# Where the tiles with direct denominators stand in a unit, who may use the denominators' PSUM bank, and the order of a row's value products

## The chip, the cores and the metric

One core of one Trainium2 chip runs the whole kernel. The metric is the device time of one execution in microseconds (us). Three runs of the kernel before took 4312.58, 4318.01 and 4329.15 us; the median is 4318.01 us. One more execution was recorded by the hardware profiler; all durations below are from it.

## The reference

Two graph attention layers over one random adjacency of 2048 nodes, for 8 independent inputs (called batches here) of 2048 x 256, in fp32. Cut to what matters:

```python
# layer 0: 8 heads of 32 columns; scores are a sum of two vectors
x_proj = einsum('bnd,hdf->bhnf', x, W)
e = leaky_relu(e_src[..., :, None] + e_dst[..., None, :], 0.2) + beta * log(adj + 1e-6)
attn = softmax(where(adj > 0, e, lowest), axis=-1)          # 2048 x 2048 per head
x = layernorm(x + (attn @ x_proj, heads joined) @ W_out.T)
# layer 1: one head; scores are a product of two matrices
h1, h2, h3 = x @ W1, x @ W2, x @ W3
e = where(adj > 0, leaky_relu(h1 @ h2.T, 0.2), -1e12)
x = layernorm(x + relu(softmax(e) @ h3))
```

## The kernel before

**Two layers at once.** Layer 0 of batch b+1 and layer 1 of batch b run side by side, b = 0 to 6; layer 0 of batch 0 runs alone first (about 526 us), and layer 1 of batch 7 alone last (about 300 us). The seven stretches between are called batches below. At the start of each, a *seam* (`seam`, line 956) turns layer 0's result into layer 1's inputs.

**Layer 0: units, tiles, strips.** A batch has eight units (four head pairs times two halves of the rows, `unit`, line 796). A unit goes through 16 tiles `jt` of 128 neighbours. For each head of the pair, a tile is made as a 128 x 1024 block of unnormalised attention in a slot of a ring of seven (`ring`, 1 MB each): VectorE takes max(c, re) and multiplies with the mask (`make`, recorded at line 880). TensorE multiplies the tile with the values in four products of 32 columns that run beside each other (`products`, line 442, recorded at line 445; "val"). These narrow products are called *strip* work. The sums of the rows, the denominators, are collected in one of two ways:

- In a *chain* tile, ScalarE first scales the mask (line 399), and GpSimd adds the made tile to a running sum (line 888; "sums"). At the unit's end one strip product with ones, "close", adds it up over partitions.
- A *direct* tile needs neither: VectorE reads the mask as it was loaded, and TensorE does a second strip product ("den") into the same PSUM bank that takes the close.

The list `DIRECT` (line 69) says which tiles are direct: 3, 6, 9, 12 and 15 in every unit of batches 1 to 7. The bank "den" is copied out by `dned` (line 947) after the close, and the next unit's first den product waits for that copy.

**Layer 1: rows.** For each of 16 rows `it` of 128 nodes, TensorE computes scores "e" in four blocks `c` of 512 columns (line 1091), ScalarE writes each through a leaky ReLU into one row buffer `p` (line 1097), VectorE subtracts the mask and takes the maximum (line 1136, "mask"), ScalarE takes the exponential (line 1142), and TensorE transposes the four blocks ("T", line 1165), which ScalarE copies to SBUF into one of four slots `pts` (line 1170). Eight pieces of value products ("acc", line 1184) follow, all into one PSUM bank. This is *full* work. While row it is transposed, the scores of row it+1 take its place in `p`, block by block.

**PSUM.** Two banks, `m0` and `m1`, serve e, T, acc and all of the seam; "val" and "den" have one each, and two pairs hold c. A bank given to a T or an e comes back when ScalarE has copied it out; a bank given to acc comes back only when the row's result has been added to x.

**What sets the order.** A planner written into the kernel (`Sched`, line 576) decides at build time in which order each engine gets its instructions: it simulates the engines with a price for each task, a table of slots for each kind of buffer, and a queue with priorities per engine. The order on each engine is then fixed; on the chip, semaphores hold an instruction until its inputs are there. Full work on TensorE is kept in the order in which the loop at line 1235 creates it. Strip work comes between by `choose_pe` (line 599): it compares the tiles already eaten with a goal, and lets a strip in at a lag over 1.5 tiles where the next full task is marked `easy`, over 4 where it is not, or whenever the next full task is not ready for 0.35 us. Every change between full and strip costs a flat 0.13 us in the plan (`TURN`, line 511). A task marked `lock` (the mask, line 1143) waits in the plan for the end of GpSimd's current instruction.

The order of a row in the seven batches comes from these lines: one T, one piece of acc, one e, one piece of acc, and so on, with the last pieces after the loop.

```python
for c in range(NB):
    turn(it, c)
    if c and b + 1 < B:
        acc(it, 2 * c - 2)
    if more:
        scores(it + 1, c)
    if c and b + 1 < B:
        acc(it, 2 * c - 1)
```

In the last layer 1 (b + 1 == B) all eight pieces of acc follow after the four pairs of T and e.

Of the kernel before, what the change touches and what calls it, by code (L numbers as in the profile page):

```python
# [9 lines left out]
F32 = mybir.dt.float32  # L10
# [8 lines left out]
P = 128  # L19
# [8 lines left out]
def kernel(  # L28
# [37 lines left out]


    J2 = NT // 2
    DIRECT = [[range(NT)] * NP] + [[(3, 6, 9, 12, 15)] * NP] * (B - 1)
    SLOTS = 7  # L70

    const = ctx.enter_context(tc.tile_pool(name="const", bufs=1))
# [306 lines left out]
    class Unit:  # L379
# [67 lines left out]
        def copy_values(self):  # L447


            gat, hp, rh, lo = self.gat, self.hp, self.rh, self.hp % 2 * HP * DH  # L450
            parts = [(rh, self.val)]
            if self.b > 0 and hp == 0:
                if rh == 0:
                    gat.first = chunk.tile([P, BK], F32, tag="pt", name="first", bufs=NB)
                    nc.scalar.copy(gat.first, self.val)
                    parts = []
                else:
                    gat.ht = [whole.tile([P, N], F32, tag="heads", name="ht")]
# [49 lines left out]
            stage(at // (NP * 2), at // 2 % NP, at % 2)  # L508

    LATE = 0.15  # L510
    TURN = 0.13
    WINDOW = 8
    LOW, HIGH, STRICT = -1.0, 1.5, 4.0

    QUEUES = {"ACT": (("copy", 0.0), ("relu", 0.3), ("evict", 0.3), ("ends", 0.4), ("exp", 0.9), ("c", 0.4), ("scale", 0.45), ("norm", 0.25)),
              "DVE": (("zsum", 0.0), ("sum", 0.0), ("tinyr", 0.1), ("tinys", 0.1), ("mask", 0.3), ("tinyd", 0.1), ("stats", 0.2), ("make", 0.3)),
# [4 lines left out]
    class Slots:  # L521
# [6 lines left out]
        def at(self, n=0):  # L528
            return sorted(self.free)[n][0] if len(self.free) > n else None
# [5 lines left out]

        def give(self, end, tag):
            self.free.append((end, tag))

    class Hold:

# [35 lines left out]
    class Sched:  # L576


        def __init__(self):
            self.q = {name: [] for names in QUEUES.values() for name, _ in names}  # L580
            self.clock = {eng: 0.0 for eng in QUEUES}
            self.pe, self.kind, self.full, self.strip, self.close = 0.0, None, [], [], []
            self.work, self.eaten, self.goal = 0.0, 0, lambda w: 0.0

        def add(self, *a, **k):
# [4 lines left out]
        def choose(self, eng):  # L590

            now, cands = self.clock[eng], []
            for rank, (name, wait) in enumerate(QUEUES[eng]):
                if self.q[name]:
                    r = self.q[name][0].ready()
                    if r is not None:
                        cands.append((rank, r, wait))
            if not cands:
                return None
            t = max(now, min(r for _, r, _ in cands))  # L600
            rank, r, wait = min(c for c in cands if c[1] <= t)
# [34 lines left out]
            return v[0], v[1], 0  # L636

        def start(self, t, task):
            for h in task.takes:
                h.take()  # L640
            task.end = t + task.busy + task.late
            for h in task.frees:
                h.done(task.end)
            task.emit()
            if task.after:
                task.after()

        def run(self):

            while True:  # L650
                best = None
                for eng in QUEUES:
                    c = self.choose(eng)
                    if c and (best is None or c[0] < best[0]):
                        best = (c[0], eng, c[1])
                c = self.choose_pe()
                if c and (best is None or c[0] < best[0]):
                    best = (c[0], "PE", c)
                if best is None:
                    break  # L660
                t, eng, what = best
                if eng == "PE":
                    task = getattr(self, what[1]).pop(what[2])
                    kind = "full" if what[1] == "full" else "strip"
                    t += TURN if self.kind not in (None, kind) else 0.0
                    self.kind, self.pe = kind, t + task.busy
                    if kind == "full":
                        self.work += task.busy
                else:
                    task = self.q[what].pop(0)  # L670
                    if task.lock:
                        t = max(t, self.clock["POOL"])
                        self.clock["POOL"] = t + task.busy
                    self.clock[eng] = t + task.busy
                self.start(t, task)
# [75 lines left out]
    ctx.enter_context(tc.manual_schedule(engines={e.engine for e in (nc.sync, nc.scalar, nc.vector, nc.gpsimd)}))  # L751
    next(projections)
    S = Sched()
    bank = Slots(2, ["m0", "m1"])
    ring, mts, pts_s, hts, rows_s = (Slots(n, None, name) for n, name in ((SLOTS, "ring"), (4, "mt"), (4, "pts"), (4, "ht"), (4, "rows")))
    v_s, c_s, pen_s, xs_s = (Slots(n, None, name) for n, name in ((2, "v"), (0, "c"), (1, "pen"), (2, "xs")))

# [51 lines left out]
    def unit(b, hp, rh, vs, vhold):  # L809
# [29 lines left out]
        for jt in range(NT):  # L839
# [68 lines left out]
            if jt in u.direct:  # L908
                def den(jt=jt):
                    e = gat.re[:, 1]  # L910
                    if u.den is None:
                        u.den = pacc.tile([P, BK], F32, tag="den", name="den")
                    u.products(u.den, [e[:, jt, h:h + 1].to_broadcast([P, DH]) for h in u.heads], u.s[jt],
                               jt == min(u.direct), False)
                deps = [u.makes[jt, 0], u.makes[jt, 1]]
                if jt == min(u.direct) and before:
                    deps.append(before.dned)
                t2 = pe("strip", "den", 0.86, lambda _, den=den: den(), deps)
                t2.frees = [slot]
                t = t2  # L920
            count = t

            def eat():
                S.eaten += 1
            t.after = eat
        u.closed = pe("close", "close", 0.86, lambda _: u.products(u.den, [ones] * HP, u.sums, False, True),
                      [u.adds[u.chain[-1], 0], u.adds[u.chain[-1], 1], t])
        if hp == 0 and rh == 0:
            hold = Hold(pts_s, 1)
            E.first_hold = hold  # L930
            u.evicted = S.add("evict", 0.5, u.copy_values, [u.vals[NT - 1]], takes=[hold])
        else:
            n = 4 if hp == 0 else 2
            deps = [u.vals[NT - 1]]
            frees = []
            if hp == 0:
                frees = [E.first_hold]
                deps.append(entries[b - 1].last_tr)
            if hp == HP and rh == 0:
                deps.append(entries[b - 1].last_tr)  # L940
            u.evicted = S.add("evict", 0.55 * n, u.copy_values, deps, frees=frees)
        dn = Hold(hts, 1)

        def dn_copy():
            u.dn = chunk.tile([P, BK], F32, tag="ht", name="dn", bufs=4)
            nc.scalar.copy(u.dn, u.den)
        u.dned = S.add("evict", 0.5, dn_copy, [u.closed], takes=[dn])
# [106 lines left out]
    def layer1(b):  # L1054
# [50 lines left out]
        def soft(it):  # L1105
# [33 lines left out]
            def exp():  # L1139
                p = pbox["p"]  # L1140
                r["den"] = den = small.tile([P, 1], F32, name="den1")
                nc.scalar.activation(p, p, AF.Exp, bias=r["neg"], accum_out=den)  # L1142
# [15 lines left out]
        def turn(it, c):  # L1158
# [8 lines left out]
            def cp(t):  # L1167
                pt = chunk.tile([P, BK], F32, tag="pt", name="pts", bufs=NB)
                r["pts"].append(pt)
                nc.scalar.copy(pt, t)  # L1170
# [64 lines left out]
        for it in range(NT):  # L1235
# [31 lines left out]
        layer1(b)  # L1267
    u = U["last"]
    u.evicted.after = lambda: bank.give(u.evicted.end, "val")
    u.dned.after = lambda: bank.give(u.dned.end, "den")  # L1270
# [34 lines left out]
```

## Time and profile before

| | |
|---|---|
| profiled execution | 4315.08 us, span 4313.3 us |
| median of three runs | 4318.01 us |
| mean granted TensorE clock | 0.985 |
| busy: TensorE, VectorE, ScalarE, GpSimd | 95%, 76%, 68%, 66% of the span |
| one batch (the fourth, 494 us): TensorE, VectorE, ScalarE, GpSimd | 474.88, 407.50, 367.37, 413.33 us |
| one make, one scale, one add | 1.27, 1.14, 2.5 us |
| one mask: beside GpSimd, and in the last layer alone | 3.44, 2.29 us (medians) |
| copies of T and e from PSUM | 0.58 and 0.59 us |

An instruction's busy time on TensorE overlaps the next one's, so the busy share says little about how near TensorE is to its own pace; the distance between the starts of two matmuls does. "PE" is TensorE's products, "PEld" its weight loads, "DVE" VectorE, "ACT" ScalarE, "POOL" GpSimd. A wait is written at the instruction that waited, with the one that released it.

### The profile page before, as it was taken

What the parts mean: (1) busy time and instruction counts of PE and PEld (TensorE: products, weight loads), DVE (VectorE), ACT (ScalarE), POOL (GpSimd) and SP (SyncE); (2) the same over time, 40 slices, a digit from 0 to 9 for tenths busy, and PEclk for the clock granted to TensorE, in tenths of its full rate; (3) what the DMA queues carried; (4) which work ended last, traced back from release to release, by engine and by line L of the source; (5) the groups of instructions that cost most, each with busy time, mean ns of one, the idle gap of its engine ahead of it and who ended that gap; (6) DMA issues with size and microseconds to landing.
All of it is one profiled execution on the core that took longest, in us unless ns stands there. A gap on an engine that the chain in (4) does not pass through costs nothing.

```text
span 4313.3 us, 60790 instructions
## 1 busy us (share of the span) xinstructions
PE 4076.4 (95%) x22704; PEld 2114.0 (49%) x22704; DVE 3297.6 (76%) x3391; ACT 2930.5 (68%) x4148; POOL 2854.5 (66%) x1190
## 2 busy tenths in 40 slices
PE   7899799999999999998999999999999999999999
PEld 4444344445444454444444454444544445445666
DVE  7888698888788778778888787887887887885222
ACT  6522478877767777776777777776777777776454
POOL 0000399987877888877888787987778868876000
PEclk9999899999999999999999999999999999999999
DMA  8888777766555665556566565565655565653111
GB/s 263 276 287 289 243 234 249 230 225 228 190 179 192 199 210 185 188 188 197 185 205 194 184 223 183 197 203 179 209 188 189 185 216 180 198 178 123 59 51 41
DMA packets 346441, 843.66 MB, mean 196 GB/s; under 512 B 49697, under 2 KB 166433, under 8 KB 346145
## 3 DMA queue, kind: packets, MB, share of 16 engines
q1 hardware_dynamic: 346144, 839.77, 59.6%
q8 instruction: 178, 2.92, 0.3%
q14 instruction: 119, 0.97, 0.1%
HBM read 763.76 MB, written 75.37 MB: 195 GB/s over the span
## 4 chain that ended last, share of the span: by engine, by line
PE 54%; ACT 14%; DVE 9%; DMA 7%; issue 4%; POOL 1%; SPq 0%; ACTq 0%; DVEq 0%; POOLq 0%
PE e L1091 17%; PE acc L1184 15%; PE val L445 10%; ACT s L399 6%; DMA mt<-mt_d 6%; DVE p L1136 5%; PE T L1165 4%; PE den L445 4%; DVE s L880 3%; PE h L1041 2%; PE h L1067 2%; ACT p L1097 2%; ACT p L1142 2%; ACT pts L1170 1%; POOL sums L888 1%
## 5 line engine op out<-in xcount | busy, mean ns | idle before, releaser
L888 POOL TENSOR_TENSOR sums<-sums,s 128x1024 f32<-128x1024 f32 x1008 | 2488.5, 2507 | 248.2 <-DVE s L880 207.6
L880 DVE SCALAR_TENSOR_TENSOR s<-c,re,s 128x1024 f32<-128x1024 f32 x1232 | 1507.0, 1273 | 112.5 <-ACT c L829 58.6
L399 ACT ACTIVATE s<-mt,re 128x1024 f32<-128x1024 f32 x1232 | 1366.4, 1145 | 185.1 <-DMA mt<-mt_d 92.3
L445 PE MATMUL val<-s,v 128*32 128x512 f32 x8192 | 1036.2, 601 | 36.4 <-DVE s L880 12.2
L1184 PE MATMUL acc<-h,pts 128*128 128x256 f32 x4096 | 1031.9, 385 | 27.0 <-ACT p L1097 26.5
L1091 PE MATMUL e<-x1t,h 128*128 128x512 f32 x2048 | 1000.1, 613 | 20.7 <-ACT pts L1170 17.9
L1184 PEld LDWEIGHTS acc<-h,pts 128*128 128x128 f32 x4096 | 747.4, 191 | 372.6 <-issue 231.7
L1136 DVE CUSTOM_DVE_ANT_0 p<-p,pen 128x2048 f32<-128x2048 f32 x128 | 460.4, 3597 | 533.0 <-ACT p L1097 532.8
L880 DVE SCALAR_TENSOR_TENSOR s<-c,re,mt 128x1024 f32<-128x1024 f32 x560 | 692.9, 1275 | 63.3 <-PE den L445 25.9
L1091 PEld LDWEIGHTS e<-x1t,h 128*128 128x128 f32 x2048 | 363.2, 192 | 424.7 <-issue 274.0
L1097 ACT ACTIVATE p<-e 128x512 f32<-128x512 f32 x512 | 303.7, 593 | 381.8 <-PE e L1091 379.1
L445 PEld LDWEIGHTS val<-s,v 128*32 128x32 f32 x8192 | 232.7, 109 | 568.3 <-issue 446.2
L888 POOL TENSOR_TENSOR sums<-s 128x1024 f32<-128x1024 f32 x112 | 270.4, 2436 | 263.2 <-DVE s L880 254.0
L445 PE MATMUL den<-s,re 128*32 128x512 f32 x3264 | 442.5, 595 | 0.0
L1165 PE MATMUL T<-ident,p 128*128 128x128 f32 x2048 | 325.3, 283 | 92.7 <-ACT p L1142 67.2
L1142 ACT ACTIVATE p<-p,neg 128x2048 f32<-128x2048 f32 x128 | 256.2, 2001 | 197.0 <-DVE neg L1137 196.9
L1165 PEld LDWEIGHTS T<-ident,p 128*128 128x128 f32 x2048 | 238.4, 142 | 306.9 <-ACT p L1142 98.0
L1170 ACT COPY pts<-T 128x512 f32<-128x512 f32 x512 | 296.7, 580 | 89.3 <-PE T L1165 88.6
L413 DVE SCALAR_TENSOR_TENSOR s<-c_in,re,mt 128x1024 f32<-128x1024 f32 x256 | 310.5, 1278 | 52.0 <-DMA mt<-mt_d 39.4
L286 POOL PARTITION_ALL_REDUCE top<-top x8 | 6.6, 820 | 429.6 <-DVE top L285 414.6
L445 PEld LDWEIGHTS den<-s,re 128*32 128x32 f32 x3264 | 107.7, 110 | 239.5 <-issue 235.8
L277 ACT COPY v<-proj 128x512 f32<-128x512 f32 x64 | 37.2, 585 | 192.8 <-PE proj L275 144.5
(100 smaller groups left out, 2467.9 us busy)
## 6 DMA issues: line engine op xcount, KB each, us to landing
mt<-mt_d SPq DMA_DIRECT2D x992, 512.0 KB
c_in<-c_d SPq DMA_DIRECT2D x64, 1024.0 KB
pen<-pen_d SPq DMA_DIRECT2D x112, 512.0 KB
xg<-in_x_dram SPq DMA_DIRECT2D x60, 512.0 KB
adj_t<-in_adj_dram SPq DMA_DIRECT2D x16, 1024.0 KB
mt_d<-mt SPq DMA_DIRECT2D x32, 512.0 KB
rb<-rec_d SPq DMA_DIRECT2D x128, 128.0 KB
adj_r<-in_adj_dram SPq DMA_DIRECT2D x32, 512.0 KB
```

The lines of the kernel that those rows point to most:

```text
L399: nc.scalar.activation(self.s[jt][:, a], self.mt[jt], AF.Copy, scale=self.gat.re[:, 1, jt, h:h + 1])
L413: nc.vector.scalar_tensor_tensor(s[:, a], self.c[a], self.gat.re[:, 0, jt, h:h + 1], m, ALU.max, ALU.mult)
L445: nc.tensor.matmul(dst[ts(q, DH), :], weights[q % 2], s[:, q % 2, ts(q // 2, BK)], start=start, stop=stop)
L880: nc.vector.scalar_tensor_tensor(u.s[jt][:, a], u.c[a], gat.re[:, 0, jt, h:h + 1], m, ALU.max, ALU.mult)
L888: nc.gpsimd.tensor_tensor(u.sums[:, a], of[:, a], u.s[jt][:, a], ALU.add)
L1091: nc.tensor.matmul(t, box["h"][:, kc, ts(it % IG, P)], gat.x1t[:, kc, ts(c, BK)], start=(kc == 0), stop=(kc == KC - 1))
L1097: nc.scalar.activation(pbox["p"][:, ts(c, BK)], t, AF.Prelu, alpha=ALPHA)
L1136: nc.vector.tensor_tensor_reduce(p, p, r["pen"], 1.0, -FMAX, ALU.subtract, ALU.max, neg)
L1142: nc.scalar.activation(p, p, AF.Exp, bias=r["neg"], accum_out=den)
L1165: nc.tensor.transpose(t[:, ts(k, P)], pbox["p"][:, ts(c * IG + k, P)], ident)
L1170: nc.scalar.copy(pt, t)
L1184: nc.tensor.matmul(r["acc"], r["pts"][g][:, ts(k, P)], gat.h3[:, j, :], start=(j == 0), stop=(j == NT - 1))
```

## The change

Four things change in code, and some prices of the planner with them.

1. `DIRECT`: the direct tiles of a unit are 11 to 15 in place of 3, 6, 9, 12 and 15. There are still five, and eleven chain tiles, now 0 to 10.
2. The bank "den" joins `m0` and `m1` in the planner's pool (`Banks`). It may be lent to any T, e, acc or seam task from the moment a unit's last tile has been eaten and `dned` has freed it until tile 8 of the next unit has been eaten; it is taken only when no other bank is free. A unit's first den product then has to take that very bank (`Only`).
3. A row of the seven batches is ordered as in the last layer: T0 e0 T1 e1 T2 e2 T3 e3, then all eight acc. Strips are easy before T0, acc 0 and acc 7.
4. The buffer `first`, which holds the first unit's values for one unit, leaves the four `pts` slots for the four `ht` slots.

In the planner, the change cost between tasks gets a table by pair and only counts where TensorE has no gap; the mask counts as ready only when GpSimd's current instruction is over, so other VectorE work may go first; its price falls from 2.4 to 2.35 us, with 0.5 us of lateness. The function that takes the mask and the minimum's sign is the same in both kernels: the sign is already taken on VectorE (line 1137).

```diff
-    DIRECT = [[range(NT)] * NP] + [[(3, 6, 9, 12, 15)] * NP] * (B - 1)
+    DIRECT = [[range(NT)] * NP] + [[(11, 12, 13, 14, 15)] * NP] * (B - 1)
...
-                    gat.first = chunk.tile([P, BK], F32, tag="pt", name="first", bufs=NB)
+                    gat.first = chunk.tile([P, BK], F32, tag="ht", name="first", bufs=4)
...
-    TURN = 0.13
+    TURN = {False: 0.0, True: 0.14, ("T", "acc"): 0.11, ("acc", "T"): 0.05, ("acc", "e"): 0.08, ("e", "acc"): 0.085, ("T", "e"): 0.04,
+            ("e", "T"): 0.03, ("e", "val"): 0.12, ("T", "val"): 0.13, ("acc", "val"): 0.08, ("val", "e"): 0.19, ("tr", "h3"): 0.1}
+    NOW = [0.0]
+    BACK = 2
...
+    class Banks(Slots):
+        def mine(self):
+            return sorted(f for f in self.free if self.lent or f[1] != "den")
...
+        def take(self):
+            f = self.mine()
+            got = min(f, key=lambda x: (x[0] > NOW[0], x[1] == "den", x[0]))
+            self.free.remove(got)
+            return got[1]
...
+            mask = self.q["mask"][0].ready() if self.q["mask"] else None
+            if False:
+                return None
...
+                        if name == "mask":
+                            r = max(r, self.clock["POOL"])
...
-                    t += TURN if self.kind not in (None, kind) else 0.0
-                    self.kind, self.pe = kind, t + task.busy
+                    if t <= self.pe + 0.05:
+                        t += TURN.get((self.last, task.queue), TURN[kind != self.kind])
+                    self.kind, self.last, self.pe = kind, task.queue, t + task.busy
...
-    bank = Slots(2, ["m0", "m1"])
+    bank = Banks(["m0", "m1", "den"])
...
-                if jt == min(u.direct) and before:
-                    deps.append(before.dned)
+                if jt == min(u.direct):
+                    u.den_hold = Hold(Only(bank, "den"), 1)
+                    t2.takes = [u.den_hold]
...
+                bank.lent = min(u.direct) - BACK > jt + 1 or jt == NT - 1
...
-            hold = Hold(pts_s, 1)
+            hold = Hold(hts, 1)
...
-        u.dned = S.add("evict", 0.5, dn_copy, [u.closed], takes=[dn])
+        u.dned = S.add("evict", 0.5, dn_copy, [u.closed], takes=[dn], frees=[u.den_hold])
...
-            mk = S.add("mask", 2.4, mask, [e.reader for e in r["e"]] + pen, frees=[pen_hold], lock=True)
+            mk = S.add("mask", 2.35, mask, [e.reader for e in r["e"]] + pen, frees=[pen_hold], lock=True, late=0.5)
...
-            t = pe("full", "T", 0.46, tr, [r["exp"]], Hold(bank, 1), ("copy", 0.5, cp, []), easy=(c < 2))
+            t = pe("full", "T", 0.46, tr, [r["exp"]], Hold(bank, 1), ("copy", 0.5, cp, []), easy=(c < 1))
...
-            t = pe("full", "acc", 0.89, mm, deps, hold, easy=(h > 6))
+            t = pe("full", "acc", 0.89, mm, deps, hold, easy=(h == 0 or h == 7))
...
-                if c and b + 1 < B:
-                    acc(it, 2 * c - 2)
...
-                if c and b + 1 < B:
-                    acc(it, 2 * c - 1)
...
-            for h in range(6 if b + 1 < B else 0, 8):
+            for h in range(8):
```

More of the change, by code (lines that the diff above doesn't have):

```diff
@@ L537, in give, with __init__, at, take @@
             self.free.append((end, tag))
+    class Banks(Slots):
+        def __init__(self, tags):
+            super().__init__(len(tags), tags)
+            self.lent = False
+        def mine(self):
+            return sorted(f for f in self.free if self.lent or f[1] != "den")
+        def at(self, n=0):
+            f = self.mine()
+            return f[n][0] if len(f) > n else None
+        def take(self):
+            f = self.mine()
+            got = min(f, key=lambda x: (x[0] > NOW[0], x[1] == "den", x[0]))
+            self.free.remove(got)
+            return got[1]
+    class Only:
+        def __init__(self, slots, tag):
+            self.slots, self.tag = slots, tag
+        def at(self, n=0):
+            return next((f[0] for f in self.slots.free if f[1] == self.tag), None)
+        def take(self):
+            self.slots.free.remove(next(f for f in self.slots.free if f[1] == self.tag))
+            return self.tag
+        def give(self, end, tag):
+            self.slots.give(end, tag)
     class Hold:
@@ L581, in __init__ @@
             self.clock = {eng: 0.0 for eng in QUEUES}
-            self.pe, self.kind, self.full, self.strip, self.close = 0.0, None, [], [], []
+            self.pe, self.kind, self.last, self.full, self.strip, self.close = 0.0, None, None, [], [], []
             self.work, self.eaten, self.goal = 0.0, 0, lambda w: 0.0
@@ L638, in start @@
         def start(self, t, task):
+            NOW[0] = t
             for h in task.takes:
@@ L915, in unit, with eat @@
                 deps = [u.makes[jt, 0], u.makes[jt, 1]]
-                if jt == min(u.direct) and before:
-                    deps.append(before.dned)
                 t2 = pe("strip", "den", 0.86, lambda _, den=den: den(), deps)
                 t2.frees = [slot]
+                if jt == min(u.direct):
+                    u.den_hold = Hold(Only(bank, "den"), 1)
+                    t2.takes = [u.den_hold]
+                    u.den_first = t2
                 t = t2
             count = t
-            def eat():
+            def eat(jt=jt):
                 S.eaten += 1
+                bank.lent = min(u.direct) - BACK > jt + 1 or jt == NT - 1
             t.after = eat
@@ L1269 @@
     u.evicted.after = lambda: bank.give(u.evicted.end, "val")
-    u.dned.after = lambda: bank.give(u.dned.end, "den")
     for a in range(HP):
```

## The prediction

> **What bounds the kernel now.** I read the page's head first, then the busy time by stretches, then the waits, then two pieces of the timeline.
>
> ```profile
> span 4313.3 us, 60790 instructions
> PE 4076.4 (95%) x22704; PEld 2114.0 (49%) x22704; DVE 3297.6 (76%) x3391; ACT 2930.5 (68%) x4148; POOL 2854.5 (66%) x1190
> ...
> 2046.00:2540.00 494.00, 474.88 (x2629) 240.46 (x2628) 407.50 (x420) 367.37 (x508) 413.33 (x173) 1.00 0.60 198
> 4009.00:4313.00 304.00, 292.98 (x1204) 202.82 (x1202) 71.54 (x148) 153.62 (x289) 0.00 (x0) 0.98 0.16 51
> ```
>
> The second pair of lines gives length and then busy time of PE, PEld, DVE, ACT and POOL, first of one batch, then of the last layer. TensorE seems full, but its records overlap, so I take its pace from the last layer, where it runs undisturbed and in the order that the change gives to all batches:
>
> ```profile
> 4151.92 0.60 PE L1165 MATMUL T<-ident,p 128*128 128x128 f32 x4
> 4152.35 1.88 PE L1091 MATMUL e<-x1t,h 128*128 128x512 f32 x4
> 4154.07 0.60 PE L1165 MATMUL T<-ident,p 128*128 128x128 f32 x4
> ...
> 4160.54 7.07 PE L1184 MATMUL acc<-h,pts 128*128 128x256 f32 x32
> 4167.45 1.45 PE L1067 MATMUL h<-x1t,w 128*128 128x512 f32 x3
> ```
>
> By starts, T costs 0.43 us, e 1.72, four pairs 8.62 (4151.92 to 4160.54), eight acc 6.91: 15.53 us a row. A strip product of a tile is spaced 0.86 us. A batch then needs, at this pace: 16 rows, 248.5; eight h1 at 1.72, 13.8; the seam's eight y, h3 and tr, 31; 128 val, 40 den and 8 close strips at 0.86, 151.4. Sum 444.7 us. The seven batches lie between 526 and 4009 us: 3483 / 7 = 497.6 us each. So 53 us a batch, about 375 in all, are lost between TensorE's instructions. I sorted the distances between starts, less the pace: 200 us lie between T, e and acc of a row; 33 us at 349 changes from full to strip (94 ns each) and 108 us at as many changes back (about 95 ns each, and 70 us of real waits at 52 of them, 48 of it before a T); the rest, 34 us, within strips and in the seam. The waits name the causes:
>
> ```profile
> POOL sums L888 <- DVE s L880: 457.3, 119, 13.2
> ...
> PEld e L1091 <- ACT pts L1170: 109.6, 229, 4.5
> ...
> PEld T L1165 <- ACT p L1097: 76.8, 183, 3.4
> ...
> PE T L1165 <- ACT p L1142: 61.8, 29, 11.4
> ...
> PEld acc L1184 <- ACT p L1097: 48.9, 73, 3.4
> ```
>
> An e that waits for `pts`, and a T or acc that waits for `p` of line 1097, wait for a copy to give a bank back. While acc is spread through the row, it holds one of two banks, and T and e share the other. One such wait:
>
> ```profile
> 2002.48 1.03 PE L1184 MATMUL acc<-h,pts 128*128 128x256 f32 x4
> ...
> 2002.92 2.19 ACT L399 ACTIVATE s<-mt,re 128x1024 f32<-128x1024 f32 x2 [2.31 <-DMA mt<-mt_d]
> 2005.02 0.57 ACT L1097 ACTIVATE p<-e 128x512 f32<-128x512 f32 x1
> ...
> 2005.64 0.33 PE L1165 MATMUL T<-ident,p 128*128 128x128 f32 x1 [2.14 <-ACT p L1097]
> ```
>
> ScalarE runs two late scales ahead of e's copy, and TensorE stands for 2.14 us with no second bank.
>
> **What the Trainium skill says.** *Perfetto Trace Analysis*, section Identifying the Most-Contended Engine: the matmul busy share is a bad measure of headroom; the trace agrees, 95% busy against 444.7 of 497.6 us (89%). The same page, Matmuls: independent groups should rotate through PSUM banks, so that the copying of one overlaps the next; the waits above show the lack of it. *TensorEngine Tiling (Array Packing)*, Key Properties: a change of tiling mode drains the array; here strip and full change for 94 + 95 ns. *SBUF — State Buffer*, SBUF: two separate sides: a VectorE instruction with two SBUF inputs and a GpSimd one exclude each other; the mask's median is 3.44 us beside GpSimd, 2.29 in the last layer.
>
> **The change, part by part.** Instructions, bytes and shapes stay: five direct tiles a unit, 20 adds, the same transfers on SP's queue, one `vscale` a pair on POOL (the old run of tiles in steps of three was one instruction too). What changes is order.
>
> *acc in one block.* T and e then have both banks, and the lent third. For the third: T0 e0 T1 fill three banks, and e1 needs T0's, whose copy has had 2.15 us; each later one has at least as long for a copy of 0.6 us. The last layer shows the order with plenty of banks: 7.7 us lost in its 253. With two banks, e(c+1) needs e(c)'s bank, covered only by T, 0.43 us, against 0.20 us until the copy starts (the median), 0.59 of copy and about 0.2 to the next matmul: a stall of 0.55 us. The bank is lent from about tile 1 to tile 8 of 16, so half the time. I take 60% of the 200 us off: -120. Ends: 0 (evictions late in both states) and -170.
>
> *The row's head.* From e3's end to the next T0 the path copy, mask, exponential takes 8.96 us (median). Before, three acc, 2.6 us, and strips covered it; now 6.9 us of acc and strips do. Half of the 48 us before T: -24; ends 0 and -40.
>
> *Strip changes.* The thresholds stay, the easy places go from T0, T1, acc 7 to T0, acc 0, acc 7: about as many clumps. I take a tenth of 349 x 0.19 us: -7; ends +15 and -25.
>
> *The mask's place.* One make, 1.27 us, may now go ahead of it and fill time in which the mask would stand for GpSimd. It lengthens the row's head by up to 1.3 us, hidden by the acc block and the strips; without that cover 112 rows x 1.3 = 146 us. Behind a mask stand makes and z's sum; they gain. 0.
>
> *`first` in `ht`.* For one unit in eight, four `pts` slots in place of three: without it T3's bank would stay taken until two acc have run. It takes a slot from h1, rb and x's loads; 0, end +10.
>
> *Direct tiles last.* This is the cost. ScalarE: a unit has 22 scales at 1.144, 25.2 us, and two c copies, 2.0; all else is 367.4 / 8 less these, 18.7 us. In the eleven chain tiles it needs 25.2 + 2.0 + 11/16 x 18.7 = 40 us of 11/16 x 60.5 = 41.6: full, where before it was evenly at 74%. Copies then come later, and late makes follow. In the half without the third bank, 112 rows x 1/2 x 4 evictions x 0.3 us (a quarter of a scale): +67. I take +65, ends 0 and +240, the latter from the second rival below.
>
> Sum: -120 - 24 - 7 + 65 = -86 us on the profiled 4313.3: span 4227, execution 4229. The median of the runs shown stands 2.9 us above the profiled 4315.08, so 4232 us (-2.0%).
>
> **The rivals.**
>
> *The lost time goes altogether.* With three banks and cover, 444.7 us plus strip changes, 9 us, and seam, 5, is 459 us a batch: -39 x 7 = -270. GpSimd speaks against the whole of it: 413 us busy of 459, 90%. With the favourable ends, -170 - 40 = -210: 4108 us.
>
> *GpSimd runs dry, and the kernel is slower.* Between the make of chain tile 10 and that of the next unit's tile 1 now stand five direct and two chain tiles: 14 makes x 1.275 = 17.9 us, with VectorE's other work (407.5 less 256 makes, 81 of 494 us) 21 us. GpSimd lives from what is waiting to be added. A unit takes it 2733.5 / 56 = 48.8 us of adds and 1.7 of the rest, 50.5 of 62.2 now. So it may idle 11.7 us a unit before it sets the period; the queue at tile 10 must hold at least 9.3 us, almost four adds. Now the adds trail their makes by 2 to 6 us only. If the queue held 7 us, idle would be 14: 56 x 2.3 = +129, 4447; empty, +520. For it: seven ring slots, three or four then held by waiting tiles. Against: eleven chain tiles in a row at 3.8 us against 5 us of adds leave 11 x 1.2 = 13 us waiting by themselves.
>
> *No difference.* Half the time there are two banks, 112 rows x 3 x 0.55 x 1/2 = 92 us of new stalls, and ScalarE's +65: these eat the 151 us. 4318.
>
> *The diff does less than its words.* The sign is on VectorE in both kernels: nothing from it, in any case.
>
> **How the numbers follow.** Forecast, 4150 to 4296: 0.57. All of the gain, under 4150: 0.15. No difference, within 0.5% (22 us, about what a measurement of this kernel can tell): 0.10. Dry GpSimd: 0.18. Faster 0.72, same 0.10, slower 0.18. The range is 4135 to 4345: it leaves out about half of the second case and most of the last, 0.2 together. The likeliest case's own range is 4150 to 4296.
>
> **What would show it.** Right: waits of e on `pts` and of T and acc on line 1097's copy under half of 235 us together; T's wait on the exponential under 40 us; a batch near 485 us; T, e, T, e in all rows. ScalarE's scales bunched, POOL idle about once a unit, in or after tiles 11 to 15. Wrong: POOL's wait for makes well over 457 us with a batch over 498 (the second rival); T and e waiting as long as before, now in the second half of each unit (the third); new waits of scales or makes on ring slots.

## The result, and the profile after

| | median, us | runs | ratio to before (95%) |
|---|---|---|---|
| before | 4317.72 | 20 | |
| after | 4322.78 | 20 | 1.0013 (0.9989 to 1.0037) |

The change makes no difference that can be measured. The forecast was 4232 us, with 4135 to 4345 as range and 0.72 on faster. The measured time lies in the range, but the outcome is "no difference", which the forecast gave 0.10. (Ratios here and below leave out runs more than 1.5% above the fastest of their kernel: two of the twenty after, and eleven of the 22 of one kernel below.)

The two kernels do not lose their time at the same places. In the profiled execution (4324.23 us) the seven stretches, from the first transpose of one seam to that of the next, take 582.8, 489.8, 490.4, 490.0, 476.8, 497.2 and 469.1 us; before they take 512.2, 502.9, 505.2, 493.4, 494.7, 505.4 and 469.3. Six stretches gain 58 us together and the first loses 71. (In the profile before, the first seam's first transpose starts at 536.8 us and the last seam's at 4019.9; the prediction laid the same 3483 us 11 us too early.)

The busy time of the first three stretches of the kernel after (length, then PE, PEld, DVE, ACT, POOL, with TensorE's clock, the share of the DMA engines and GB/s at the end):

```profile
533.00:1116.00 583.00, 509.23 (x2762) 253.00 (x2763) 480.33 (x454) 398.26 (x536) 447.14 (x185) 0.95 0.61 207
1116.00:1606.00 490.00, 468.96 (x2628) 247.13 (x2626) 413.18 (x412) 364.52 (x506) 402.09 (x168) 0.99 0.59 198
1606.00:2096.00 490.00, 470.59 (x2623) 246.16 (x2621) 413.07 (x419) 367.07 (x509) 411.24 (x171) 0.99 0.59 200
```

In the first stretch TensorE stands still for 74 us of 583, and its granted clock falls to 0.95. The waits of the whole kernel after (engine and line, who released it, us in total, times, longest):

```profile
POOL sums L934 <- DVE s L926: 511.7, 77, 20.8
...
DVE s L926 <- ACT s L399: 289.0, 282, 11.1
...
PEld val L445 <- DVE s L926: 135.6, 122, 23.0
...
PE T L1214 <- ACT p L1191: 66.5, 25, 9.5
...
PEld e L1140 <- ACT p L1146: 57.4, 75, 3.6
...
PEld T L1214 <- ACT pts L1219: 26.5, 55, 2.4
...
PEld e L1140 <- ACT pts L1219: 16.8, 20, 0.9
PEld acc L1233 <- ACT pts L1219: 3.5, 10, 0.8
PEld T L1214 <- ACT p L1146: 2.5, 7, 0.8
```

Two things stand out. The waits for a bank fell: the three kinds that came to 235 us before come to 19 now. New ones stand in their place, e behind the copy of the last e (57.4) and T behind the copy of an earlier T (26.5); with these and the small ones on both sides, T, e and acc wait 107 us for copies where they waited 257. That part of the forecast came. And a strip product waits up to 23.0 us for a make, where before the longest wait of a val for a make of this kind was 11.1 us. This is the longest one, in three engines of the timeline:

```profile
639.76 30.07 POOL L934 TENSOR_TENSOR sums<-sums,s 128x1024 f32<-128x1024 f32 x13
...
650.13 21.86 DVE L1185 CUSTOM_DVE_ANT_0 p<-p,pen 128x2048 f32<-128x2048 f32 x1
...
672.11 2.47 DVE L926 SCALAR_TENSOR_TENSOR s<-c,re,s 128x1024 f32<-128x1024 f32 x2
...
645.50 5.83 PE L445 MATMUL val<-s,v 128*32 128x512 f32 x22 [1.30 <-DVE s L926]
673.45 3.06 PE L445 MATMUL val<-s,v 128*32 128x512 f32 x8 [22.12 <-DVE s L926]
```

GpSimd runs thirteen adds without a gap, until 669.8. VectorE's mask starts at 650.13 and needs 2.28 us when it is alone; it takes 21.86, ends 2.2 us after the run has ended, and the makes queued behind it on VectorE start only then. TensorE stands for 22 us. A second mask of 16.3 us, at 591.5, stops TensorE for 17 us in the same stretch. Over the seven stretches, the masks' durations (shortest, median and longest in ns), before and then after:

```profile
L1136 DVE CUSTOM_DVE_ANT_0 p<-p,pen x112: 2281/3440/14412, 599.5 to 3990.6; 128x2048 f32<-128x2048 f32 x112
```

```profile
L1185 DVE CUSTOM_DVE_ANT_0 p<-p,pen x112: 2277/3132/21855, 591.5 to 4000.1; 128x2048 f32<-128x2048 f32 x112
```

The median even falls; the tail grows. A mask alone takes 2.28 us and the rest of one add at most 2.4, so I call a mask over 5 us *passed over*: at least one further add went ahead of it. That happened to 12 of 112 masks before and to 11 after. In all 23 cases the mask came in only when GpSimd's run of adds had come to an end, never at a later boundary inside the run (in two, before, a `vscale` followed that run within 0.5 us and stood behind the mask). In 20 of the 23, what let GpSimd go on, by the releasers that the profile gives, was a VectorE instruction that stood behind the mask, mostly a make: the run ended because GpSimd had nothing left to add. Before, one to five adds went ahead, 2.1 on average; after, up to eight, 3.6 on average. GpSimd's instructions in the seven stretches follow one another without a gap of 0.15 us in runs of 6.8 on average before and 10.4 after. So masks are passed over about as often, and the length of the runs became the price.

### The profile page after: what moved, and what is told of

It is laid out like the page before. It is cut to its first block, busy times and chain, and to the rows that moved or that the text cites. A ratio compares the mean times of both kernels' runs of the same rounds, so it can differ in the third digit from the quotient of the medians.

```text
span 4322.1 us, 60882 instructions
## 1 busy us (share of the span) xinstructions
PE 4045.2 (94%) x22704; PEld 2157.3 (50%) x22704; DVE 3358.5 (78%) x3391; ACT 2914.6 (67%) x4148; POOL 2861.0 (66%) x1190
## 4 chain that ended last, share of the span: by engine, by line
PE 54%; DVE 14%; ACT 10%; issue 7%; DMA 2%; POOL 1%; SPq 0%; ACTq 0%; DVEq 0%; POOLq 0%
PE e L1140 17%; PE acc L1233 13%; PE val L445 11%; DVE s L926 7%; DVE p L1185 5%; ACT s L399 5%; PE den L445 4%; PE T L1214 4%; PE h L1090 3%; PE h L1116 2%; POOL sums L934 1%; ACT p L1146 1%; ACT p L1191 1%; PE y L1031 1%; DMA mt<-mt_d 1%
## 5 line engine op out<-in xcount | busy, mean ns | idle before, releaser
L445 PE MATMUL val<-s,v 128*32 128x512 f32 x8192 | 1047.3, 601 | 95.6 <-DVE s L926 68.5
L1233 PE MATMUL acc<-h,pts 128*128 128x256 f32 x4096 | 924.0, 381 | 0.4 <-ACT pts L1219 0.4
L1233 PEld LDWEIGHTS acc<-h,pts 128*128 128x128 f32 x4096 | 770.0, 190 | 215.5 <-issue 93.2
L926 DVE SCALAR_TENSOR_TENSOR s<-c,re,mt 128x1024 f32<-128x1024 f32 x560 | 678.8, 1274 | 38.5 <-POOL sums L934 28.4
L1185 DVE CUSTOM_DVE_ANT_0 p<-p,pen 128x2048 f32<-128x2048 f32 x128 | 483.1, 3774 | 210.4 <-ACT p L1146 209.4
L1214 PEld LDWEIGHTS T<-ident,p 128*128 128x128 f32 x2048 | 254.5, 144 | 344.5 <-issue 177.3
L1214 PE MATMUL T<-ident,p 128*128 128x128 f32 x2048 | 317.2, 280 | 73.6 <-ACT p L1191 66.5
L1249 ACT ACTIVATE acc<-acc,rec 128x256 f32<-128x256 f32 x128 | 56.7, 443 | 190.7 <-PE acc L1233 184.6
```

What stands on the lines that cost most here:

```text
L445: nc.tensor.matmul(dst[ts(q, DH), :], weights[q % 2], s[:, q % 2, ts(q // 2, BK)], start=start, stop=stop)
L926: nc.vector.scalar_tensor_tensor(u.s[jt][:, a], u.c[a], gat.re[:, 0, jt, h:h + 1], m, ALU.max, ALU.mult)
L1185: nc.vector.tensor_tensor_reduce(p, p, r["pen"], 1.0, -FMAX, ALU.subtract, ALU.max, neg)
L1214: nc.tensor.transpose(t[:, ts(k, P)], pbox["p"][:, ts(c * IG + k, P)], ident)
L1233: nc.tensor.matmul(r["acc"], r["pts"][g][:, ts(k, P)], gat.h3[:, j, :], start=(j == 0), stop=(j == NT - 1))
```

## The experiments

My theory after this comparison: the change gains what it should on TensorE's banks, and gives it back because chain tiles in a row make GpSimd's adds run without a gap, so that a mask that is passed over waits for the end of a long run. Rivals: ScalarE, which now has to scale eleven tiles in a row (the makes' wait for scales rose from 52.7 to 289 us); GpSimd as a bound; and the planner's new place for the mask, which starts 4.6 us after the last copy of e on average where it was 0.1.

All ratios below are to the kernel before, measured beside each kernel, with a 95% interval.

### A GpSimd that stands still for the mask

The edit leaves the order of all other instructions as it is:

```diff
                 nc.vector.tensor_scalar(neg, neg, -1.0, None, ALU.mult)
+                turn_off = small.tile([P, 1], F32, name="yield", bufs=2)
+                nc.gpsimd.tensor_tensor(turn_off, neg, neg, ALU.add)
```

GpSimd reads the mask's result, so its queue stops at this place until the mask is done. I call it the yield. In the kernel after:

> The kernel after, with one small GpSimd instruction behind each mask of the rows (it adds the mask's 128 x 1 result to itself, into a tile that nothing reads), so that GpSimd's queue stops there until the mask is done; the order on all engines is otherwise the same. Theory (the lost gain went into masks that wait while GpSimd runs a long row of adds): no mask over 4.8 us (one of 2.3 plus the rest of one add), no stall of 17 or 23 us in the first of the seven stretches, that stretch near 530 us in place of 583, the whole 50 to 80 us shorter, near 4255. Rival (the scales of eleven chain tiles in a row saturate ScalarE, and the makes wait for them): time unchanged within 10 us, the makes' wait for scales still near 289 us. Second rival (GpSimd is the bound): slower, since it now stands before each mask.

In the kernel before:

> The kernel before, with the same small GpSimd instruction behind each mask. Theory: masks over 4.8 us (41 us beyond that in the profile before, longest 14.4) go, and with them part of the waits before a T: 20 to 40 us shorter, near 4288, less than in the kernel after. Rival (ScalarE): unchanged. Second rival (GpSimd is the bound): slower.

Measured: after with the yield 4214.47 us, 0.9765 (0.9737 to 0.9793); before with the yield 4238.49 us, 0.9818 (0.979 to 0.9846). No mask is passed over in either. The masks of the kernel after with the yield, and the first two of its stretches:

```profile
L1185 DVE CUSTOM_DVE_ANT_0 p<-p,pen x112: 2273/2696/4448, 599.1 to 3885.0; 128x2048 f32<-128x2048 f32 x112
```

```profile
540.00:1089.00 549.00, 511.58 (x2764) 253.15 (x2763) 451.46 (x455) 398.21 (x536) 436.67 (x201) 0.97 0.66 220
1089.00:1560.00 471.00, 462.19 (x2627) 244.55 (x2625) 396.60 (x413) 364.87 (x507) 386.56 (x183) 1.00 0.61 206
```

The wait of its makes for scales:

```profile
DVE s L926 <- ACT s L399: 305.0, 299, 11.0
```

The theory holds and was too small: 108 us from the kernel after, not 50 to 80, and 79 from the one before, not 20 to 40. The first stretch falls to 549, not to 530, but the others fall too, the next two to 471 and 475 us. I had counted only the long stalls, but the yield also shortens the masks that were not passed over: the median falls from 3.13 to 2.70 us, in the kernel before from 3.44 to 2.91. All 112 masks together lose 120 us in the kernel after and 94 in the one before, and these sums are near what the times lose, 108 and 79. ScalarE as the cause falls: the makes still wait 305 us for scales here, and the time is gone all the same. GpSimd as the bound falls: it now waits 430 us for masks, and the kernel is faster. The six runs lie within 8 us of each other, where the twenty of the kernel after lie within 78: which mask is passed over seems to be drawn anew in each execution.

And against the kernel before with the yield, the change is now worth 24 us, 0.5%.

### The control: the same instruction without a wait

```diff
-                nc.gpsimd.tensor_tensor(turn_off, neg, neg, ALU.add)
+                nc.gpsimd.tensor_tensor(turn_off, eps_ln, eps_ln, ALU.add)
```

> Control for the yield: the kernel after with the same small GpSimd instruction at the same places, but reading a constant, so that it waits for no mask. Theory (it is GpSimd's standing still that lets the mask in): long masks as in the kernel after, time within 25 us of it, 4300 to 4345. Rival (any short instruction between two adds breaks the run): no mask over 4.8 us and 4214, as with the yield.

Measured: 4274.57 us, 0.9903 (0.9881 to 0.9925). Neither holds. Five masks are passed over in place of eleven, and the longest takes 11.5 us: a short instruction among the adds prevents some of it by itself, which my theory had excluded. The time falls by 48 us, where the wait takes off 108. Most of what the wait adds is seen in the masks: they take 2.91 us on average with the yield and 3.30 with the control, 0.39 x 112 = 44 of the 60 us between the two.

### The parts of the change one by one

The value products in one block alone, in the kernel before:

```diff
             for c in range(NB):
                 turn(it, c)
-                if c and b + 1 < B:
-                    acc(it, 2 * c - 2)
                 if more:
                     scores(it + 1, c)
-                if c and b + 1 < B:
-                    acc(it, 2 * c - 1)
...
-            for h in range(6 if b + 1 < B else 0, 8):
+            for h in range(8):
```

(with the two `easy` edits of the change)

> The kernel before, with the value products of a row in one block and the places for strips that go with it, and nothing else: two banks, direct tiles spread. Prediction's third rival: T and e now wait for each other's bank, waits of T and e on copies stay at 150 us or more, time 4320 to 4350. Prediction's forecast: acc no longer holds a bank through the row, which is worth more than that: 4270 to 4300.

Measured: 4276.25 us, 0.9899 (0.9868 to 0.993). The time is the forecast's, but the waits are the rival's: e alone waits 235 us for copies, 121 for `pts` and 114 for the copy of the last e. So the gain does not come from the banks. The same with the yield:

> The kernel before, with the value products in one block and the yield. If the block is worth here what it is worth without the yield (36 us of 4312): near 4202. If the whole worth of the change with the yield, 24 us, is the block's: near 4214. If the block's gain was that of fewer waits behind long masks: near 4238.

Measured: 4234.28 us, 0.9819 (0.9789 to 0.9849): the same as the kernel before with the yield, 0.9818. The third reading holds. Without passed-over masks the block is worth nothing under two banks; what it gained without the yield has to do with late masks. Its one profile shows seven passed over where the kernel before has twelve, but all masks together are only 19 us shorter, of 36 us gained. And the yield takes 77 us off the masks here and only 42 off the time: the block covers part of a late mask. (The waits of e for the copy of the last e stand at 111 us with the yield too, a wait that the interleaved order did not have: the prediction's third rival, in part. And the block has 435 changes between strip and full in place of 349.)

The direct tiles last alone, in the kernel before, without and with the yield:

```diff
-    DIRECT = [[range(NT)] * NP] + [[(3, 6, 9, 12, 15)] * NP] * (B - 1)
+    DIRECT = [[range(NT)] * NP] + [[(11, 12, 13, 14, 15)] * NP] * (B - 1)
```

> The kernel before, with the direct tiles at 11 to 15 and nothing else. Theory (chain tiles in a row make GpSimd's adds run without a gap, and a mask that comes then waits for the end of the run): more masks over 8 us than the kernel before has, 4340 to 4390. Rival (ScalarE's scales in a row are the cost): also 4340 to 4390, so the next run decides between them. If neither holds: 4300 to 4320.

> The same with the small GpSimd instruction behind each mask. Theory: the cost of the direct tiles' place is nearly all in the long masks, so this is within 15 us of the kernel before with the yield, 4225 to 4255. Rival (ScalarE): stays 20 to 60 us above that, 4260 to 4300.

Measured: 4424.9 us, 1.0263 (1.0222 to 1.0304), and 4251.42 us, 0.9854 (0.9825 to 0.9883). This pair decides between GpSimd's runs and ScalarE. Direct tiles last cost 106 us of 4319 alone, more than I expected, and at most some 13 us with the yield (4251 against 4238; the intervals, 0.9825 to 0.9883 and 0.979 to 0.9846, overlap). In the profile without the yield 18 masks are passed over, by up to six adds, 3.6 on average; 13 masks take over 8 us, where the kernel before has four. The exponential (line 1142) waits 338 us for the masks, 197 in the kernel before:

```profile
POOL sums L888 <- DVE s L880: 614.9, 85, 32.4
...
ACT p L1142 <- DVE neg L1137: 338.4, 91, 18.8
...
DVE s L880 <- ACT s L399: 243.2, 282, 11.0
```

```profile
L1136 DVE CUSTOM_DVE_ANT_0 p<-p,pen x112: 2278/3282/18065, 595.0 to 4108.5; 128x2048 f32<-128x2048 f32 x112
```

With the yield the masks lose 186 us together and the time 173. The makes' wait for scales is 243 us without the yield and 251 with it. It cost at most the 13 us that are left.

The planner's rule and price for the mask, put back in the kernel after, without and with the yield:

```diff
-                        if name == "mask":
-                            r = max(r, self.clock["POOL"])
...
-            mk = S.add("mask", 2.35, mask, [e.reader for e in r["e"]] + pen, frees=[pen_hold], lock=True, late=0.5)
+            mk = S.add("mask", 2.4, mask, [e.reader for e in r["e"]] + pen, frees=[pen_hold], lock=True)
```

> The kernel after, with the planner's old rule and price for the mask: it is ready when its inputs are, whatever GpSimd does, so no make goes ahead of it for that reason. Theory: the mask starts at once after the last copy of e (4.6 us later on average in the kernel after), the path from e to T shortens by some 4 us, but acc and strips covered it mostly: 0 to 30 us shorter, 4295 to 4325; long masks remain. Rival (the deferral itself is what ate the gain): 50 us shorter or more.

> The kernel after, with the old rule and price for the mask and the yield. With the yield the mask waits for one add at most, so the make that the new rule lets ahead of it buys little and delays the exponential: 10 to 30 us below the kernel after with the yield, near 4195. If the acc block covers the delay in full: 4214 as with the new rule.

Measured: 4309.76 us as the median of 22 runs, which reach from 4249 to 4405, and 4287.16 as that of the eleven in the ratio, 0.9938 (0.9911 to 0.9965). With the yield: 4206.93 us, 0.975 (0.9721 to 0.978). Without the yield the old rule is 13 us below the kernel after by the one median and some 34 by the other; with so wide a spread no closer figure can be given, but the rival's 50 us do not come. With the yield the 7.5 us to the new rule are less than the 10 to 30 expected, and the intervals overlap: the deferral of the mask is mostly covered, as the prediction said. The first stretch alone shows it, 533 us in place of 549.

### The lent bank

Block, direct tiles last and yield under the old planner, so without the lending, without the new prices and with `first` among the `pts` slots:

> The kernel before with the value products in one block, direct tiles last and the yield, under the old planner: no lent bank, no new prices, the buffer first among the pts slots. Against the kernel after with the old mask rule and the yield (ratio 0.975) it leaves out the lending, the table of change costs and first's move. If the lending is what makes the order pay: near 4250, ratio 0.985, as direct tiles last alone with the yield. If it is not: near 4207.

Measured: 4260.6 us, 0.9867 (0.9844 to 0.9889): the order does not pay without the lending. Two more runs part the lending from the prices. The first keeps all of the change but the table, with the old mask rule and the yield; the second puts only the table into the kernel of 4260.6 us:

```diff
-                    if t <= self.pe + 0.05:
-                        t += TURN.get((self.last, task.queue), TURN[kind != self.kind])
+                    t += TURN if self.kind not in (None, kind) else 0.0
```

(with `TURN = 0.13`; the second is this diff the other way round)

> The kernel after with the old mask rule and the yield (ratio 0.975), and with the old flat price of 0.13 us for every change between strip and full: so the block, the direct tiles last, first among the ht slots and the lent bank, and no new prices. If the lending carries the gain over the same order without it (0.9867): 0.975 within 0.004, 4190 to 4225. If the prices carry it: 0.985 or above, 4250.

> The other way round: block, direct tiles last, yield and the new table of change prices in the kernel before, without the lent bank. If the lending carries the gain: 0.9867 within 0.004, 4245 to 4280. If the prices carry it: near 0.975, 4210.

Measured: 4186.78 us, 0.9689 (0.9665 to 0.9714), and 4275.67 us, 0.9897 (0.9873 to 0.9921). The lending, with `first` moved, carries the gain: 0.9867 to 0.9689, 77 us. (Lending without the block, and `first` moved without the lending, were not run.) The new prices are no help. With the lending they cost 0.6%, which neither expectation had; without it they cost 0.3%, within the intervals. The largest waits for a bank, all of e, without the lending and then with it:

```profile
PEld e L1091 <- ACT pts L1172: 107.4, 122, 4.6
PEld e L1091 <- ACT p L1097: 100.5, 171, 3.3
```

```profile
PEld e L1138 <- ACT p L1144: 37.0, 55, 4.4
...
PEld e L1138 <- ACT pts L1219: 18.5, 18, 4.0
```

T, e and acc together wait 224 us for copies without the lending and 86 with it. With the yield, then, the parts stand in a row: 4238 us before, 4261 with the block and the direct tiles last, 4187 with the lending, 4207 with the new prices, 4214 with the new rule for the mask.

### The first stretch

The first of the seven stretches also reads the adjacency and makes masks of it, on slots that the rest uses too. This kernel (the one after with the old mask rule and the yield) has its direct tiles spread there as before:

```diff
-    DIRECT = [[range(NT)] * NP] + [[(11, 12, 13, 14, 15)] * NP] * (B - 1)
+    DIRECT = [[range(NT)] * NP] + [[(3, 6, 9, 12, 15)] * NP] + [[(11, 12, 13, 14, 15)] * NP] * (B - 2)
```

> The kernel after with the old mask rule and the yield, and with the direct tiles at 3, 6, 9, 12 and 15 in the first of the seven stretches alone, which takes 549 us against 514 in the kernel before with the yield. If the direct tiles' place is what the first stretch suffers from[...]: 20 to 35 us shorter, near 4180. If not: 4207.

Measured: 4186.07 us, 0.969 (0.9663 to 0.9716): 21 us shorter, the low end of what was expected. The first stretch takes 513 us, 20 fewer than with the old mask rule and the yield alone. Why the direct tiles' place costs so much there is not shown. This kernel and the one with the lending and the old prices are both 3.1% faster than the kernel before; the two edits were not run together.

### A probe of the mask beside a run of adds

Appended to the kernel before, on scratch tiles (names shortened):

```diff
+    for n in (0, 1, 2, 3, 4, 5, 6, 8, 10, 12, 16, 20):
+        nc.gpsimd.tensor_tensor(go, token, token, ALU.add)
+        for k in range(9):
+            nc.gpsimd.tensor_tensor(a[:, k % 2], a[:, k % 2], b[:, k % 2], ALU.add)
+        nc.vector.tensor_scalar(fill, go, -1.0, None, ALU.mult)
+        for k in range(n):
+            nc.vector.bn_stats(st, y[:, 0:256])
+        nc.vector.tensor_tensor_reduce(y, y, pm, 1.0, -FMAX, ALU.subtract, ALU.max, token)
```

> The kernel before, followed by twelve rounds of a probe on scratch data: nine 128 x 1024 adds on GpSimd that wait only for one another, and on VectorE 0 to 20 statistics of 128 x 256 (one SBUF input, 0.43 us each) and then one mask; each round starts when the mask before is done. Theory: the mask either gets in at the first end of an add after its start, about 2.3 to 4.7 us long, or at the end of the run, up to 20 us, and nothing between. Rival (each end of an add is a fresh draw): durations at every step of 2.3 us.

Inconclusive. All twelve masks came in at the first end of an add, in 2.29 to 3.90 us; none was passed over, so the probe shows no wait for a run's end. It does show the other side of the exclusion: the add behind such a mask stands for it and takes 4.38 us in place of 2.33. One round, whose five adds take 13.57 us:

```profile
4347.52 13.57 POOL L1287 TENSOR_TENSOR probe<-probe 128x1024 f32<-128x1024 f32 x5
...
4348.45 3.56 DVE L1294 CUSTOM_DVE_ANT_0 probe<-probe,penm 128x2048 f32<-128x2048 f32 x1
```

The probe's adds wait only for one another, those of the kernel also for VectorE's makes. What decides whether a mask is passed over stays open; neither the time from its start to the end of the running add nor the spacing of the adds told the two kinds apart in the trace of the kernel before. There 77 masks met a running add with a GpSimd instruction ready behind it, and 12 of them were passed over; with direct tiles last it was 18 of 87, after the change 11 of 80.

## Why the prediction was wrong

The seven stretches by TensorE's distances between starts, less the pace, in us. Here single losses over 3 us stand apart, so the columns differ a little from the prediction's.

| | seven stretches | over 3 us | in rows (T, e, acc) | strip to full | full to strip | within strips | seam |
|---|---|---|---|---|---|---|---|
| before | 3483.1 | 51.1 | 178.6 | 84.2 | 32.9 | 10.9 | 23.9 |
| after | 3496.0 | 121.4 | 108.1 | 63.8 | 28.7 | 29.5 | 33.6 |
| before, yield | 3407.4 | 20.0 | 157.8 | 60.8 | 32.6 | 10.3 | 24.5 |
| after, yield | 3373.7 | 31.5 | 79.3 | 56.5 | 28.4 | 35.4 | 30.8 |
| block, last, yield, no lending | 3427.7 | 33.6 | 131.2 | 72.5 | 40.9 | 19.7 | 25.8 |
| lending, old prices, yield | 3359.4 | 39.4 | 80.3 | 49.2 | 29.4 | 18.1 | 38.1 |

(What is left to the total is the pace itself, 3101 to 3112 us.)

- **acc in one block, and the lent bank: -120.** The mechanism was right for the two together, the size too large: 70 us came off inside the rows. With the yield it is 78. But I put the block and the lending into one term and gave the block alone a share. The block alone gives nothing once masks are not passed over; the gain comes with the lending.
- **The row's head: -24.** Strip to full fell by 20, but T's wait on the exponential did not fall; with the yield strip to full falls by 4. This term was not parted from the late masks. (The parts that the prediction gives for its 108 us of these changes, 33 and 70, make 103.)
- **Strip changes: -7.** From 349 changes to 303, and full to strip fell by 4.
- **The mask's place: 0.** For the new rule in the plan the 0 was nearly right, 7.5 us with the yield, though the mask starts 4.6 us later on average and not up to 1.3. But I named the exclusion of VectorE and GpSimd here, saw the median of 3.44 us, and did not look at the tail: the longest mask before had 14.4 us, and 12 were passed over. The yield, which takes these away and shortens the others, is worth 79 us in the kernel before.
- **Direct tiles last: +65, laid to ScalarE.** This is the step that failed: the cost of the edit was laid to ScalarE's scales and copies, and the mask's wait behind GpSimd's run of adds was put at nothing. ScalarE's lateness came (289 us of waits for scales) and cost at most some 13 us. What the edit costs alone is 106 us, and nearly all of that goes when GpSimd stands still for the mask. In the whole change it shows as +70 us in losses over 3 us, just what the rows had gained (with the yield these losses are 31.5 in place of 121.4); losses within strips and at the seam, +28, and 10 in the count of the pace outweigh the 25 that the strip changes gained.
- **The rivals.** "GpSimd runs dry" asked how long GpSimd would stand still between two units; the harm lay in its not standing still while a mask waits. A sign of that rival came all the same, GpSimd's waits for makes of 512 us and a first stretch of 583: the makes were late behind the masks. "No difference" named the right time for a wrong reason: T and e were to wait as before, and they wait less than half as long. That the time came out the same is chance: the gain and the loss, each about 70 us, have different causes.

Of what the prediction set down as signs, the waits for banks under half of 235 us came true (19 for the waits named, 107 of 257 for all), and so did stretches near 485 us, as the mean of the last six (486). T's wait on the exponential, called to fall under 40 us, stayed at 66.5 against 67.2 over the whole kernel: that line told of the failed step. With the yield it is 22.7.

## What to carry to other kernels

Where an instruction on one engine takes longer beside another engine's work, look at its longest duration and at the length of the other's unbroken run, not at the median: here an order that kept GpSimd fed without a gap starved VectorE. Give the engine with slack an instruction that waits for the one on the critical path; here one add of 128 x 1 behind each mask is worth 1.8% in one kernel and 2.5% in the other. And when a change of several parts moves nothing, run the parts: here one cost 2.6% alone, another gave 1.0% alone but nothing with the yield, and a third took off 1.8% with the yield.

## What the runs showed of the hardware

- The mask, a VectorE instruction with two SBUF inputs, either came in at the end of the GpSimd add that it met or waited for the end of the whole run. In the traces of the kernels before, after and with direct tiles last, 41 masks of 336 took over 5 us, with one to eight further instructions of 2.3 us ahead of them (adds, but for two multiplies of the same size), and all of them came in only when the run of adds had ended. (Five others ended within 5 us though an add had begun within 0.4 us after them.) The makes, which read one tensor from SBUF and one from PSUM, stay between 1.18 and 1.30 us in the trace before. The section of the Trainium skill that the prediction cites (*SBUF — State Buffer*, SBUF: two separate sides) says that whichever of the two starts first has the pair for its whole instruction, which fits the masks that came in at the end of an add; it does not say who is next. That it is the port is inferred from the durations, the page and the yield; no run shows the port itself.
- A short GpSimd instruction of 128 x 1 behind each mask in GpSimd's order, without any wait, cut the passed-over masks from eleven to five, in one profile of each kernel.
- While TensorE stood for 22 us, its granted clock fell to half (0.50 from 656 us on in the trace after) and came back some 3 us after it resumed (673.5 to 676 us). In the stop of 17 us at 592.6 us it fell at 598 and came back at 615, some 6 us after TensorE resumed.
